# One tag per slot for the big PSUM tiles and the exps tiles of a fused ViT layer

## The chip, the cores and the metric

The kernel runs on one core of one Trainium2 chip. The metric is the device time of one execution in microseconds (us). Before the change, three runs gave 3957.31, 3959.95 and 3960.58 us; the median is 3959.95 us.

## What is computed

A small vision tower: patches are turned into tokens, and one layer with attention and a mixture of experts follows. There are 16 images of 512x512, with 1024 tokens of width 256 each, all in float32. Cut to what matters here:

```python
h = patches(x) @ W.T + b                        # tokens
q, k, v = split(layernorm(h) @ w_qkv)           # 8 heads of 32
k = sum_f a_f * sin(f * k) + b_f * cos(f * k)   # 256 frequencies
attn = softmax(q @ k.T * 32 ** -0.5)
h = h + (attn @ v) @ w_out + b_out
n = layernorm(h)
h = h + shared_mlp(n) + sum of the two best of four experts, weighted by their gates
```

## The kernel before

One long unrolled program handles the 16 images. Its function `plain_path` holds everything that follows; a second path for extreme inputs stands behind a branch and is not taken here.

**The key transform.** The keys of a pair of heads are worked on in 8 groups, 512 groups in all (16 images, 4 pairs of heads, 8 groups). For a group, the angles come in by DMA (`load_waves`, L1072) or are spread by VectorE from one loaded tile (`spread_waves`, L1112). GpSimd multiplies them by the frequencies (`turn_waves`, L1127), ScalarE takes the sines (`sine`, L1136), TensorE weighs them with the coefficients in a *mix* (`mix`, L1156, 16 matmuls into one big PSUM tile called `kan`), and VectorE multiplies the mix by the fast sines (`times_fast`, L1170). TensorE then adds up the products of two groups (`add_up`, L1189, tile `red`), and after four of those the keys of the pair are split and stacked by DMA (`finish_keys`, L1208, and `stack_keys`, L1218).

**Attention.** There are 128 attentions (4 pairs of heads by 2 halves of the queries by 16 images) of 8 chunks `kc` each, so 1024 *scores*. A score (`score`, L1254) is two matmuls into a big PSUM tile `sT` of 128x1024. ScalarE takes the exp (`exponential`, L1270): for an even `kc` it goes to a tile `es` in SBUF, which frees the PSUM tile; for an odd `kc` it stays in place in PSUM. VectorE then adds the odd chunk in PSUM to the even one in SBUF (`pair_sum`, L1285), the result `both` goes to SBUF, and only then is the odd chunk's PSUM tile free. TensorE weighs the values with `es` (8 matmuls) and with `both` (16 matmuls, sums included) in `weigh` (L1300, tile `av`). VectorE divides by the sums (L1324, L1329, L1341).

**The rest.** Tokens, layernorms (VectorE statistics, a chain of small GpSimd steps L621 to L625, ScalarE L633, transposes on TensorE L454), projections and networks are spread between these steps by four chains of generators. They use their own two PSUM slots, `side0` and `side1`, taken through one tag each.

**The slots that the change touches.** Mixes and scores share two PSUM slots of 4 KB per partition: pool `big` (L263) has two buffers under one tag, `big`. `es` and `both` share five SBUF slots: pool `esp` (L258) has NES = 5 buffers under one tag, `es`. With several buffers under a tag, the framework gives a new tile one of the slots when it lays out the program, and makes the tile's first writer wait for the last users of that slot.

**What sets the order of the work.** The order of the instructions of each of the five engines is written out in strings, `ORDERS` (L73 to L225): for TensorE, M is a mix, R an `add_up`, S a score, W a weighting, and digits are steps of the chains. A planner (`run`, L582) walks through them with estimated costs and emits each action. For TensorE, `head` (L564) lets a mix or a score begin in the plan when the user of the last but one big tile is done; the list `bigs` (L1145) holds those users, and `lay_fixed` (L550) adds to it just before the action is called:

```python
at = begin(PE, deps + (bigs[-2:-1] if user_of(token, key) else []))
```

In the same way `tile_free` (L1275) lets an exps tile wait, in the plan, for the weighting of the tile five before it, and for the pair sum too where that one was even.

## Time and profile before

| | |
|---|---|
| median of three runs | 3959.95 us |
| the profiled execution's own time | 3963.14 us |
| its span, first to last instruction | 3961.6 us |
| granted TensorE clock, mean | 0.985 |
| scores, matmuls (L1254) | 2048, 461 ns each |
| mixes, matmuls (L1156) | 8192, 603 ns each |
| exp to `es` (L1270, even chunks) | 512, 1022 ns each |
| exp in place (L1270, odd chunks) | 512, 1012 ns each |
| pair sum (L1285) | 512, 1221 ns each |
| product of a mix (L1170) | 512, 1215 ns each |
| HBM traffic | 230 GB/s over the span |

In the profile, PE is TensorE's matmuls and PEld its weight loads, which overlap with them; DVE is VectorE, ACT ScalarE, POOL GpSimd, SP SyncE. A line such as `av<-es,v` names what is written and what is read. Brackets at the end of a line of the timeline give the idle time of that engine before the instruction and what ended it. In the tables of waits, the columns are the total in us, the number of times, and the longest in us. The first score comes at 142.2 us, the last at 3886.3 us; between some 1000 and 3300 us one image follows the other with a period of about 236 us.

### The profile page before, as it was taken

The numbers are of one execution on the slowest core, as the hardware profiler recorded it, in microseconds if no ns is written. First come the engines' busy times: TensorE is split into PE (matmuls) and PEld (weight loads), VectorE is DVE, ScalarE is ACT, GpSimd is POOL, SyncE is SP. The second block draws the span as 40 slices with busy tenths as digits, with TensorE's granted clock in tenths as the row PEclk, the third lists the DMA queues.
The fourth block names the chain that finished last, engine by engine and source line by source line (L and its number), as shares of the span: only waits on it lengthen the run. The fifth ranks groups of instructions, "written<-read, shape, count | busy, mean of one in ns | idle before, by whom it ended". The sixth has DMA issues, their size and how long they took to land. (4 is left out here: it accounts for less than half of the span.)

```text
span 3961.6 us, 95230 instructions
## 1 busy us (share of the span) xinstructions
PE 3714.6 (94%) x36493; PEld 1784.6 (45%) x36493; DVE 3119.1 (79%) x4715; ACT 3319.6 (84%) x3927; POOL 3193.0 (81%) x2312
## 2 busy tenths in 40 slices
PE   7888999999999999999999999999999999999988
PEld 4324344454444544454454444444454454443434
DVE  4777878878787787878888787887878888797763
ACT  2789988898888888888888888888888898989883
POOL 4988878888888888888888878888888888888850
PEclk9999999999999999999999999999999999999999
DMA  7887977788788788889879788887878878788750
GB/s 241 266 250 210 258 209 230 242 219 273 204 247 253 219 257 224 260 225 252 248 219 279 211 247 243 225 262 215 260 229 247 260 218 261 221 238 232 226 151 18
DMA packets 587586, 916.03 MB, mean 231 GB/s; under 512 B 58828, under 2 KB 177524, under 8 KB 587124
## 3 DMA queue, kind: packets, MB, share of 16 engines
q1 hardware_dynamic: 580880, 906.98, 79.4%
q8 instruction: 291, 4.77, 0.5%
q10 hardware_dynamic: 6244, 2.88, 0.3%
q14 instruction: 171, 1.40, 0.1%
HBM read 758.64 MB, written 150.99 MB: 230 GB/s over the span
## 5 line engine op out<-in xcount | busy, mean ns | idle before, releaser
L1127 POOL TENSOR_TENSOR w<-w,lane 128x1024 int32<-128x1024 int32 x1024 | 1926.8, 1896 | 303.5 <-DMA w<-ud 204.8
L1127 POOL TENSOR_TENSOR f<-f,lane 128x1024 int32<-128x1024 int32 x512 | 970.8, 1896 | 173.1 <-DVE f L1112 131.6
L1136 ACT ACTIVATE w<-w 128x1024 f32<-128x1024 int32 x1024 | 1016.3, 1047 | 57.5 <-POOL w L1127 54.7
L1254 PE MATMUL sT<-q,k 128*128 128x512 f32 x2048 | 739.8, 461 | 138.2 <-ACT es L1270 61.2
L1285 DVE TENSOR_TENSOR both<-sT,es 128x1024 f32<-128x1024 f32 x512 | 625.1, 1221 | 306.0 <-ACT sT L1270 298.7
L1170 DVE TENSOR_TENSOR f<-kan,f 128x1024 f32<-128x1024 f32 x512 | 610.8, 1215 | 162.2 <-ACT f L1136 111.4
L1270 ACT ACTIVATE sT<-sT 128x1024 f32<-128x1024 f32 x512 | 518.0, 1012 | 234.8 <-PE sT L1254 175.4
L1112 DVE STREAM_SHUFFLE f<-src 128x1024 int32<-128x1024 int32 x512 | 691.0, 1362 | 0.9
L1270 ACT ACTIVATE es<-sT 128x1024 f32<-128x1024 f32 x512 | 523.1, 1022 | 105.9 <-PE sT L1254 82.3
L1254 PEld LDWEIGHTS sT<-q,k 128*128 128x128 f32 x2048 | 346.0, 192 | 542.6 <-ACT es L1270 161.8
L1156 PE MATMUL kan<-w,coef 64*32 64x512 f32 x8192 | 558.1, 603 | 31.6 <-ACT w L1136 15.8
L1136 ACT ACTIVATE f<-f 128x1024 f32<-128x1024 int32 x512 | 516.1, 1045 | 0.2
L1300 PE MATMUL av<-both,v 128*32 128x256 f32 x4096 | 324.3, 387 | 3.0 <-DVE both L1285 2.9
L1300 PE MATMUL av<-es,v 128*32 128x256 f32 x4096 | 324.4, 388 | 2.2 <-DVE rc L1341 2.1
L1300 PE MATMUL av<-both,ones 128*32 128x256 f32 x4096 | 320.4, 383 | 0.0
L1189 PE MATMUL red<-f,pack 128*32 128x512 f32 x2048 | 288.2, 605 | 13.4 <-DVE f L1170 13.0
L1324 DVE RECIPROCAL rc<-av 128x256 f32<-128x256 f32 x128 | 224.1, 1751 | 55.4 <-PE av L1300 54.2
L1156 PEld LDWEIGHTS kan<-w,coef 64*32 64x32 f32 x8192 | 119.3, 105 | 303.5 <-issue 114.0
L445 PE MATMUL tok<-wt,x 128*128 128x256 f32 x1008 | 234.7, 384 | 13.8 <-DMA x<-in_xT 12.3
L445 PEld LDWEIGHTS tok<-wt,x 128*128 128x128 f32 x1008 | 189.9, 191 | 61.2 <-issue 21.5
L1136 ACT ACT_TABLE_LOAD x154 | 197.6, 1283 | 21.4 <-DMA w<-ud 18.7
L1300 PEld LDWEIGHTS av<-both,v 128*32 128x32 f32 x4096 | 115.5, 110 | 174.7 <-issue 111.7
(161 smaller groups left out, 4773.3 us busy)
## 6 DMA issues: line engine op xcount, KB each, us to landing
w<-ud SPq DMA_DIRECT2D x2048, 256.0 KB
q<-qd SPq DMA_DIRECT2D x512, 128.0 KB
k<-kd SPq DMA_DIRECT2D x128, 512.0 KB
x<-in_xT SPq DMA_DIRECT2D x128, 384.0 KB
ud<-u SPq DMA_DIRECT2D x64, 512.0 KB
ud<-ui SPq DMA_DIRECT2D x64, 512.0 KB
src<-ud SPq DMA_DIRECT2D x512, 64.0 KB
qd<-qhi SPq DMA_DIRECT2D x64, 256.0 KB
```

The costliest lines, as they stand in the source:

```text
L445: nc.tensor.matmul(out=out, lhsT=lhsT, rhs=rhs, start=start, stop=stop)
L1112: nc.vector.stream_shuffle(w, sources[g // 8].rearrange("p r n -> p (r n)"), [4 * (g % 8) + i // 8 for i in range(32)],)
L1127: nc.gpsimd.tensor_tensor(w, w, f.to_broadcast([P, N]), ALU.mult)
L1136: nc.scalar.activation(x, w, AF.Sin, scale=TURN * 2.0**-32)
L1156: nc.tensor.matmul(out=ps[ds(64 * j + 32 * blk, 32), ts(r, 512)], lhsT=coef[ts(r, 64)].rearrange("p e f j -> p (e f j)"), rhs=w[ts(r, 64), ...
L1170: nc.vector.tensor_mul(w, kan.pop(g), w)
L1189: nc.tensor.matmul(out=rows_of_pair[p][ts(2 * i + r, 32), :], lhsT=pack[:, ds(PACK0 - 16 * (k % 2) - 2 * (k // 2), 32)], rhs=prod[:, ts(r, ...
L1254: nc.tensor.matmul(out=ps[:, ts(s, 512)], lhsT=k4[:, 2 * s + kc // 4, ts(kc % 4, P)], rhs=q4[:, s, :], start=True, stop=True,)
L1270: nc.scalar.activation(es, ps, AF.Exp, scale=SCALE)
L1285: nc.vector.tensor_add(both, scores[kc], exps[kc - 1])
L1300: nc.tensor.matmul(out=acc[0][ts(i, HD), ts(half, 256)], lhsT=ones32 if half else v[:, kc, p % NPAIR, ts(i % 2, HD)], rhs=es[:, ds(512 * ( ...
L1324: nc.vector.reciprocal(rc[0], acc[0][:, 256:512])
```

## The change

The two big slots and the five exps slots each get a tag of their own with one buffer, and the program names the tag. A mix or score takes `big0` and `big1` alternately, by the number of takings so far. An `es` or `both` tile takes slot `(att * NT + kc) % NES`, with NT = 8 chunks per attention. Number and size of the slots stay, as do the instruction orders.

```diff
-    esp = pool("esp", NES)
+    esp = pool("esp", 1)
...
-    big = pool("big", 2, PSUM)
+    big = pool("big", 1, PSUM)
...
-            ps = kan[g] = big.tile([P, N], FP, tag="big", name="kan")
+            ps = kan[g] = big.tile([P, N], FP, tag=f"big{len(bigs) % 2}", name="kan")
...
-            ps = scores[kc] = big.tile([P, 1024], FP, tag="big", name="sT")
+            ps = scores[kc] = big.tile([P, 1024], FP, tag=f"big{len(bigs) % 2}", name="sT")
...
-                es = exps[kc] = esp.tile([P, 1024], FP, tag="es", name="es")
+                es = exps[kc] = esp.tile([P, 1024], FP, tag=f"es{(att * NT + kc) % NES}", name="es")
...
-            both = exps[kc] = esp.tile([P, 1024], FP, tag="es", name="both")
+            both = exps[kc] = esp.tile([P, 1024], FP, tag=f"es{(att * NT + kc) % NES}", name="both")
```

## The prediction

> **What bounds the kernel now.** I read the page's busy times first, then the stretches of one image, then who waited for whom, and last the instructions around the slots.

> ```profile
> PE 3714.6 (94%) x36493; PEld 1784.6 (45%) x36493; DVE 3119.1 (79%) x4715; ACT 3319.6 (84%) x3927; POOL 3193.0 (81%) x2312
> ```
> ```profile
> core 0: us, PE busy (x) PEld busy (x) DVE busy (x) ACT busy (x) POOL busy (x), PEclk, DMA share, GB/s
> 1666.00:1902.00 236.00, 227.85 (x2307) 112.07 (x2306) 195.83 (x296) 203.30 (x244) 199.83 (x144) 0.99 0.86 242
> ```

> In the steady part one image takes 236 us, of which TensorE (PE) is busy 227.85. Only 8.1 us per image is idle there, so a slot rule can win only part of that, and anything that holds PE up costs nearly its full length. The chain that ended last covers only the tail (PE 2% of the span), so I go by PE's waits.

> ```profile
> PE sT L1254 <- ACT es L1270: 61.2, 51, 4.4
> PE sT L1254 <- DVE both L1285: 22.6, 33, 3.0
> PE kan L1156 <- ACT es L1270: 4.6, 7, 1.1
> ```

> The columns are total us, times, longest us. A score (sT) needs no result of an exp. When it waits for one, it waits for the slot that the exp reads. These are the waits that the change touches: 61.2 us in all, the largest row of PE's waits.

> **Which slot is taken now.** The trace has no slot numbers, so I put all 1536 takings of a big slot (512 mixes, 1024 scores) in order of start and gave each the end of its last user: the product (L1170) for a mix, the exp for an even score, the pair sum (L1285) for an odd score. In strict turn, taking n may not start before the user of n-2 is done. 114 takings start earlier, so they took the slot of n-1: 100 are odd score, even score, odd score; 12 are odd score, even score, mix. In the first pattern 187 of some 356 wait on ScalarE's semaphore and 158 on VectorE's, so about half go out of turn. This is one such case:

> ```profile
> 1786.96 1.02 ACT L1270 ACTIVATE es<-sT 128x1024 f32<-128x1024 f32 x1
> 1787.08 1.23 DVE L1285 TENSOR_TENSOR both<-sT,es 128x1024 f32<-128x1024 f32 x1 [0.41 <-ACT sT L1270]
> 1788.21 0.76 PEld L1254 LDWEIGHTS sT<-q,k 128*128 128x128 f32 x4 [0.41 <-ACT es L1270]
> ```

> Two releases run side by side: the even exp ends at 1787.98, the pair sum at 1788.31. The score's weights start at 1788.21, after the exp and before the sum. In turn they would have started after the sum, 0.15 us later. Here is the opposite case:

> ```profile
> 1845.85 1.09 ACT L633 ACTIVATE hn<-h,less,rstd 128x256 f32<-128x256 f32 x2 [2.04 <-POOL less L625]
> 1846.85 1.00 ACT L1270 ACTIVATE es<-sT 128x1024 f32<-128x1024 f32 x1
> 1847.90 0.30 PEld L1254 LDWEIGHTS sT<-q,k 128*128 128x128 f32 x2 [2.61 <-ACT es L1270]
> 1847.91 0.73 PE L1254 MATMUL sT<-q,k 128*128 128x512 f32 x2 [2.42 <-ACT es L1270]
> 1848.57 0.16 PEld L1300 LDWEIGHTS av<-both,v 128*32 128x32 f32 x8 [0.37 <-issue]
> 1848.73 1.01 ACT L1270 ACTIVATE sT<-sT 128x1024 f32<-128x1024 f32 x1 [0.87 <-ACT es L1270]
> 1849.57 0.30 PEld L1254 LDWEIGHTS sT<-q,k 128*128 128x128 f32 x2 [0.41 <-issue]
> ```

> A late layernorm (hn) delays the even exp. The score waits 2.4 us for that exp's slot, though the other slot had been free since 1845.37. The same spot comes in nine images from 1139 to 3032 us, with PE idle 2.3 to 4.4 us each, 27.4 us together.

> [...] weights of a score start up to 0.56 us before the modelled end of the matmuls before. [...]

> **The change part by part.** No instruction of work is added, removed or moved; the orders of all five engines and all DMA issues stay. Only what a taking waits for changes.

> *Big slots, gain.* Where the exp of n-1 comes later than the release of n-2, the score may start earlier. I count 40 takings that start within 0.11 us of n-1's release with n-2 already free; PE idle before them is 31.9 us, of which 27.4 is the nine-fold spot. Not all is won. At 1848 the score (0.73) and the weighting (0.37 for the switch, then 0.64 and 0.61) would fill about 2.0 us; then the next even score needs the slot of that same late exp, and PE waits there for what is left (on average 27.4 / 9 - 2.0 = 1.0). What surely moves is ScalarE: its exp of the score follows the even exp at once, without the 0.87 idle in the last but one line shown. The whole trace has this row:

> ```profile
> ACT sT L1270 <- ACT es L1270: 13.0, 15, 0.9
> ```

> I take these 13.0 us as the gain (15 times 0.87), since PE's next step after the spot, a transpose (lnT), waits for four hn of ScalarE, which move by 0.87 and no more. Bounds: 0 and 31.9.

> *Big slots, loss.* For the 114 out-of-turn takings, end of n-2's user plus 0.05 us (a wait's usual lag, as 1847.85 to 1847.90) minus the start sums to 24.7 us; the median is 0.15, the longest 1.26. Part is covered: where the weights start ahead of the running matmuls, a later start costs nothing until the lead less 0.21 us (load 0.19, gap 0.02) is used up. Taken one by one, 41 with a lead of 0.45 or more lose 0.4 of 9.1 us, 22 with a lead of 0.2 to 0.45 lose 2.4 of 4.4, and the other 51 with hardly any lead, or with PE idle, lose all of their 11.2. The loss is 14.0 us. Bounds: 14.0, and 24.7 if the modelled lead is not real. Behind the waiting score stand the weightings (av), mixes and projections in PE's queue; who waits for it is ScalarE's exp (175.4 us of ACT's idle time is for sT at odd scores), then the pair sum.

> *Even score after an out-of-turn one.* Now it takes the slot of the sum; in turn it takes that of the even exp, which ended earlier or at the same time. I take nothing.

> *Exps slots.* In turn, taking m waits for the release of m-5 (weighting, and for an even tile also the sum). No exp or sum in the trace starts before that; the earliest comes 0.07 us after. 40 takings start within 0.12 us of it; at each of them the four younger tiles still hold the other slots, so that wait is forced either way (ACT es waits for PE av 38 times, 20.0 us). Cost zero, hidden by four younger tiles. An added or dropped EventSemaphore would be 0.05 us; about 100 even exps have one on VectorE now. Bounds: -5 and +5 us.

> *Sum.* How much reaches the end? PE has about ten short stalls per image. Those at 1690 (2.0, keys by DMA) and 1806 (2.0, product after a sine) depend on work that PE itself fed shortly before, so shifts mostly pass; the spot at 1848 depends on POOL's layernorm, and its remaining 1.0 us swallows losses that PE gathered since 1806. I let 0.8 of the gain and 0.65 of the loss through: -10.4 + 9.1 = -1.3 us. The profiled execution took 3963.14 us (span 3961.6 and 1.5 around it), so 3961.8 on its scale; it lies 3.2 above the median of 3959.95, which makes 3958.6, say **3959.0**. With shares from 0.5 to 1 for either, gain and loss give -6.0 to +7.5: 3953 to 3968 is the forecast's own range.

> **Rivals.**
> *Faster.* PE sets the pace, so what counts is PE's idle time: nine times 2.0 refilled and the other 4.5 us of the 31.9, against half the loss: -18.0 - 4.5 + 7.0 = -15.5, 3944. For it: PE is 97% busy in the steady part. Against it: lnT waits for hn.
> *Slower.* The pair sum becomes the only release of each odd score and adds VectorE's queue to PE's path. If the weight lead is only a modelled one, all 24.7 us count, and half of the 13.0 is swallowed: +18.2, 3978. It decides from the point at which the loss let through exceeds the gain by 7.9 us. For it: exp and sum start side by side, and the sum takes 1.22 against 1.02, so it is mostly the later one; it also stands behind reciprocals of 1.75. Against it: 41 of the 114 lie where PE still works for half a microsecond.
> *It does nothing.* If slots went in turn already, no taking could start before n-2 is free. 114 do, so this is left only with a small chance, at 3960.

> **Numbers.** Forecast 0.50, faster rival 0.24, slower rival 0.22, nothing 0.04. About 0.2% (7.9 us) is what a measurement of this kernel can tell from no change, so same is 0.54. The range reaches half into both rivals, with the 5 us of the semaphores: 3945 to 3975.

> **What would show it.** Right: no taking starts before n-2's user ends; "PE sT <- ACT es" falls from 61.2 to about 30 to 45 and "ACT sT <- ACT es" from 13.0 to near zero; "PE sT <- DVE both" rises from 22.6 by up to 14; the stall near 1848 moves to the even score, some 1 us long; "ACT es <- PE av" stays near 20. Wrong: a PE busy share per image that leaves 228 by over 1 us in 236, a new row of waits at L1285 for PE av, or a period that differs from 236 by more than 0.7 us.

## The result and the profile after

The changed kernel takes 3951.56 us in the median, beside 3965.91 us for the kernel before on the same chip, in 20 runs of each. The ratio is 0.9965 with a 95% interval of 0.9953 to 0.9978, so the change saves 0.35%, some 13.9 us (9 to 19). The time lies inside the predicted range of 3945 to 3975, but the range owes that to its width and, in part, to luck: it was laid around 3959.95 us, the median of three runs, and the twenty have a median of 3965.91. The same saving from 3959.95 would give 3946, one microsecond above the lower end. As a change, the forecast was -1.3 us and the measured one is ten times that. The likeliest case, no measurable difference, is not what happened: the kernel became faster, nearly by the -15.5 us of the first rival. The profiled execution took 3944.68 us (span 3943.1), 18.5 us less than the one before; the mean granted clock is 0.989, before 0.985.

The page after, busy time by engine, and then the stretch of one image:

```profile
PE 3710.7 (94%) x36493; PEld 1775.9 (45%) x36493; DVE 3132.7 (79%) x4715; ACT 3317.7 (84%) x3927; POOL 3190.9 (81%) x2312
```
```profile
core 0: us, PE busy (x) PEld busy (x) DVE busy (x) ACT busy (x) POOL busy (x), PEclk, DMA share, GB/s
1666.00:1902.00 236.00, 227.75 (x2307) 111.26 (x2309) 197.32 (x296) 203.27 (x243) 200.08 (x144) 1.00 0.86 243
```

The counts of matmuls, activations and vector instructions are the old ones. PE is busy only 3.9 us less, while the span shrank by 18.5, so the other 14.6 us were time in which the profile has PE idle. A fixed window of 236 us doesn't show this: the kernel now does more than one image in it. The start of one and the same score in images eight apart does: (3144.8 - 1253.5) / 8 = 236.4 us per image before, (3124.1 - 1248.8) / 8 = 234.4 after. Two microseconds over nine images are the whole of the difference between the two profiles.

PE's waits after (line, what ended the wait, us in total, times, longest):

```profile
PE sT L1254 <- ACT es L1270: 37.4, 47, 4.3
PE sT L1254 <- DVE both L1285: 32.5, 51, 3.1
```

The score's wait for an exp fell from 61.2 to 37.4, its wait for a pair sum rose from 22.6 to 32.5. ScalarE's waits at the exps after:

```profile
ACT sT L1270 <- PE sT L1254: 206.3, 222, 5.0
...
ACT es L1270 <- PE av L1300: 22.2, 38, 1.0
...
ACT sT L1270 <- ACT es L1270: 0.9, 1, 0.9
```

The last row was 13.0 us in 15 waits. The middle one, for the exps slot, is where it was (20.0). The nine-fold spot, in the image that was shown before at 1848 us, now looks so (timeline, lines of ScalarE and of PE's matmuls alone):

```profile
1839.16 1.09 ACT L633 ACTIVATE hn<-h,less,rstd 128x256 f32<-128x256 f32 x2 [1.50 <-POOL less L625]
1839.28 0.73 PE L1254 MATMUL sT<-q,k 128*128 128x512 f32 x2
1839.94 0.64 PE L1300 MATMUL av<-both,v 128*32 128x256 f32 x8
1840.16 1.00 ACT L1270 ACTIVATE es<-sT 128x1024 f32<-128x1024 f32 x1
1840.40 0.61 PE L1300 MATMUL av<-both,ones 128*32 128x256 f32 x8
1841.06 1.01 ACT L1270 ACTIVATE sT<-sT 128x1024 f32<-128x1024 f32 x1
1841.21 0.73 PE L1254 MATMUL sT<-q,k 128*128 128x512 f32 x2 [0.20 <-ACT es L1270]
```

The odd score starts at 1839.28, before the even exp (1840.16) has begun. Before, it started only after that exp. ScalarE's exp in place follows the even exp at once (1841.06), where it had an idle 0.87. PE now waits at the next, even score, here 0.20 us. Taken one by one, PE's idle time at the nine odd scores was 27.4 us before and is none after; at the nine even scores behind them it was none and is 10.7 us. PE refills 16.7 us, 1.86 at each spot; the prediction took 2.0.

### The profile page after: what moved, and what is told of

It is laid out like the page before. It is cut to its first block, busy times and chain, and to the rows that moved or that the text cites. A ratio compares the mean times of both kernels' runs of the same rounds, so it can differ in the third digit from the quotient of the medians.

```text
span 3943.1 us, 95385 instructions
## 1 busy us (share of the span) xinstructions
PE 3710.7 (94%) x36493; PEld 1775.9 (45%) x36493; DVE 3132.7 (79%) x4715; ACT 3317.7 (84%) x3927; POOL 3190.9 (81%) x2312
## 5 line engine op out<-in xcount | busy, mean ns | idle before, releaser
L1285 DVE TENSOR_TENSOR both<-sT,es 128x1024 f32<-128x1024 f32 x512 | 625.3, 1221 | 276.5 <-ACT sT L1270 265.5
L1254 PE MATMUL sT<-q,k 128*128 128x512 f32 x2048 | 727.6, 454 | 121.1 <-ACT es L1270 37.4
L1170 DVE TENSOR_TENSOR f<-kan,f 128x1024 f32<-128x1024 f32 x512 | 611.2, 1216 | 154.7 <-ACT f L1136 105.9
L1270 ACT ACTIVATE sT<-sT 128x1024 f32<-128x1024 f32 x512 | 518.1, 1012 | 219.8 <-PE sT L1254 206.3
L1270 ACT ACTIVATE es<-sT 128x1024 f32<-128x1024 f32 x512 | 522.8, 1021 | 100.8 <-PE sT L1254 75.2
L1156 PE MATMUL kan<-w,coef 64*32 64x512 f32 x8192 | 557.1, 603 | 30.5 <-ACT w L1136 13.6
L1254 PEld LDWEIGHTS sT<-q,k 128*128 128x128 f32 x2048 | 340.4, 190 | 537.2 <-DVE both L1285 158.1
L1300 PE MATMUL av<-both,v 128*32 128x256 f32 x4096 | 321.7, 384 | 4.7 <-DVE both L1285 4.7
L1300 PE MATMUL av<-es,v 128*32 128x256 f32 x4096 | 324.0, 387 | 0.9 <-DVE rc L1341 0.9
L1300 PE MATMUL av<-both,ones 128*32 128x256 f32 x4096 | 317.4, 380 | 0.0
L1156 PEld LDWEIGHTS kan<-w,coef 64*32 64x32 f32 x8192 | 118.0, 105 | 302.3 <-issue 109.2
L1300 PEld LDWEIGHTS av<-both,v 128*32 128x32 f32 x4096 | 115.5, 109 | 174.6 <-issue 110.2
```

Of the source, the lines that this page charges most:

```text
L1156: nc.tensor.matmul(out=ps[ds(64 * j + 32 * blk, 32), ts(r, 512)], lhsT=coef[ts(r, 64)].rearrange("p e f j -> p (e f j)"), rhs=w[ts(r, 64), ...
L1170: nc.vector.tensor_mul(w, kan.pop(g), w)
L1254: nc.tensor.matmul(out=ps[:, ts(s, 512)], lhsT=k4[:, 2 * s + kc // 4, ts(kc % 4, P)], rhs=q4[:, s, :], start=True, stop=True,)
L1270: nc.scalar.activation(es, ps, AF.Exp, scale=SCALE)
L1285: nc.vector.tensor_add(both, scores[kc], exps[kc - 1])
L1300: nc.tensor.matmul(out=acc[0][ts(i, HD), ts(half, 256)], lhsT=ones32 if half else v[:, kc, p % NPAIR, ts(i % 2, HD)], rhs=es[:, ds(512 * ( ...
```

## The experiments

Each kernel was timed beside the kernel before on the same chip; the ratios are to that kernel, with 95% intervals, and what stands as an uncertainty or as "within" below is a 95% interval too. No experiment alters what is computed; the dummy matmuls of two of them come on top, and nobody reads their result.

### Each half alone

The big slots by one tag each, the exps slots as before:

```diff
-    big = pool("big", 2, PSUM)
+    big = pool("big", 1, PSUM)
...
-            ps = kan[g] = big.tile([P, N], FP, tag="big", name="kan")
+            ps = kan[g] = big.tile([P, N], FP, tag=f"big{len(bigs) % 2}", name="kan")
...
-            ps = scores[kc] = big.tile([P, 1024], FP, tag="big", name="sT")
+            ps = scores[kc] = big.tile([P, 1024], FP, tag=f"big{len(bigs) % 2}", name="sT")
```

> The two big slots in strict turn, the exps slots as before. Spot theory (the gain comes from the score that waited for a late exp once per image in nine images): the whole gain is here, ratio to the kernel before 0.995 to 0.998. Exps theory (the gain comes from the exps slots): ratio within 0.001 of 1. Spread theory (many small releases of big slots): 0.995 to 0.998 as well, so this run tells only big slots from exps slots.

The exps slots by one tag each, the big slots as before:

```diff
-    esp = pool("esp", NES)
+    esp = pool("esp", 1)
...
-                es = exps[kc] = esp.tile([P, 1024], FP, tag="es", name="es")
+                es = exps[kc] = esp.tile([P, 1024], FP, tag=f"es{(att * NT + kc) % NES}", name="es")
...
-            both = exps[kc] = esp.tile([P, 1024], FP, tag="es", name="both")
+            both = exps[kc] = esp.tile([P, 1024], FP, tag=f"es{(att * NT + kc) % NES}", name="both")
```

> The five exps slots in strict turn, the big slots as before. Spot theory and spread theory: ratio 0.999 to 1.001, since every take of an exps slot in the trace of before starts after the tile five before it is free. Exps theory: 0.995 to 0.998.

Measured: big slots alone 0.9975 (0.9964 to 0.9986), exps slots alone 0.9995 (0.9983 to 1.0007). The big slots carry the gain. The exps slots give nothing that can be measured, although the layout of the compiled kernels shows that the change did alter them: counted by the number `att * NT + kc`, before 97 takings came four after the slot's last taking and 97 six after, and now all come five after.

### The nine spots out, the nine spots in

The same layouts show that the kernel before took 211 of its 1536 big slots out of turn, and the changed one none. The next three kernels choose among the 211. In the first, only the nine spots are taken out of turn as before; everything else is as in the changed kernel:

```diff
+STAYS = {
+    411, 507, 603, 699, 795, 891, 987, 1083, 1179,
+}
...
+    slot = [0]
+
+    def next_slot():
+        if len(bigs) - 1 not in STAYS:
+            slot[0] ^= 1
+        return slot[0]
...
-            ps = kan[g] = big.tile([P, N], FP, tag=f"big{len(bigs) % 2}", name="kan")
+            ps = kan[g] = big.tile([P, N], FP, tag=f"big{next_slot()}", name="kan")
...
-            ps = scores[kc] = big.tile([P, 1024], FP, tag=f"big{len(bigs) % 2}", name="sT")
+            ps = scores[kc] = big.tile([P, 1024], FP, tag=f"big{next_slot()}", name="sT")
```

> The changed kernel, but at nine scores (one in each of nine images, the spot near 1848 us of before) the slot of the last taking is used again, as the kernel before does there. Spot theory: most of the gain is gone, ratio to before 0.999 to 1.001, PE idle 2 to 4 us again at each of the nine, and the period of an image back from 234.4 to 236 us. Spread theory: more than half of the gain stays, ratio at most 0.998.

In the second, STAYS holds the other 202, so that only the nine spots are in turn:

> The kernel before's 211 out-of-turn takings kept, but the nine of the spot put in turn; exps slots in turn. Spot theory: the gain is here, and the small waits for pair sums are not paid, so ratio to before 0.993 to 0.9965, as fast as the changed kernel or up to 9 us faster. Spread theory: less than half of the gain, ratio 0.998 or more.

In the third, a control, STAYS holds all 211: the old assignment, written out by tags.

> All 211 out-of-turn takings of the kernel before, written as a list over the changed kernel, exps slots in turn: the big slots exactly as before. Spot theory: ratio to before 0.999 to 1.001, as with the exps slots alone. If some effect of the tags themselves counted, it would differ by more.

The changed kernel once more, beside the control on the same chip:

> The changed kernel once more, on the chip of the runs beside it. Ratio to before 0.995 to 0.998.

| kernel | nine spots | other 202 | ratio to before |
|---|---|---|---|
| changed | in turn | in turn | 0.9965 (0.9953 to 0.9978) |
| changed, again | in turn | in turn | 0.9970 (0.9959 to 0.9982) |
| spots in | in turn | out | 0.9963 (0.9950 to 0.9976) |
| spots out | out | in turn | 1.0002 (0.9986 to 1.0018) |
| all out | out | out | 0.9990 (0.9975 to 1.0004) |

All three rows with the spots in turn are faster, and neither of the two without. The tags by themselves give nothing (all out, 0.9990). With the others in turn, the nine spots are worth 1.0002 - 0.9970 = 0.0032, 12.7 us, with the others out 0.9990 - 0.9963 = 0.0027, 10.7 us; each difference has an uncertainty of about 0.002. These pairs stand on different chips. On one and the same chip, big slots alone (0.9975) and spots out (1.0002) differ by 0.0027, and spots in (0.9963) and exps slots alone (0.9995) by 0.0032. With the spots out, ScalarE's idle time is back, on the waits of that kernel and on its timeline (the spot of the same image):

```profile
ACT sT L1280 <- ACT es L1280: 7.9, 9, 0.9
```
```profile
1844.00 1.00 ACT L1280 ACTIVATE es<-sT 128x1024 f32<-128x1024 f32 x1
1845.06 0.30 PEld L1264 LDWEIGHTS sT<-q,k 128*128 128x128 f32 x2 [1.48 <-ACT es L1280]
1845.06 0.73 PE L1264 MATMUL sT<-q,k 128*128 128x512 f32 x2 [1.29 <-ACT es L1280]
...
1845.88 1.01 ACT L1280 ACTIVATE sT<-sT 128x1024 f32<-128x1024 f32 x1 [0.87 <-ACT es L1280]
```

The score starts 0.06 us after the exp's end, and its own exp 0.87 after it.

### Is it TensorE's clock?

A rival came up from the traces. Between 1000 and 3200 us the trace before has TensorE's granted clock at one half in 12 windows, eleven of 3.413 us and one of 6.827; the trace after has 3, of 3.413 each. 7 of the 12 begin at one of the nine spots. So PE's stall might cost by what comes after it. This kernel is the one with the spots out, with the stall filled by five dummy matmuls into the free slot:

```diff
+            if len(bigs) - 1 in STAYS:
+                warm = big.tile([P, 1024], FP, tag=f"big{slot[0] ^ 1}", name="warm")
+                for i in range(5):
+                    nc.tensor.matmul(
+                        out=warm[:, ts(i % 2, 512)],
+                        lhsT=k4[:, i % 2, 0:P],
+                        rhs=q4[:, i % 2, :],
+                        start=True,
+                        stop=True,
+                    )
```

> The changed kernel with the nine spots out of turn, and with five extra matmuls of 0.4 us each put ahead of each of the nine waiting scores, written into the other, free slot, where nobody reads them. The score still waits for the late exp; only TensorE's idle time before it is filled. Clock theory (at the spot the idle time lets TensorE's clock fall to half for 3.4 us, and that is most of what the spot costs): no half-clock windows at the nine spots, ratio to before 0.9965 to 0.9985. Queue theory (the spot costs because ScalarE's next exp comes 0.87 us late and TensorE's work lies behind it): filling helps nothing, ratio 0.999 to 1.002.

Measured: 1.0002 (0.9990 to 1.0014). Its timeline at the spot:

```profile
1844.96 1.43 PE L1265 MATMUL warm<-q,k 128*128 128x512 f32 x5
1845.61 1.00 ACT L1290 ACTIVATE es<-sT 128x1024 f32<-128x1024 f32 x1
1846.66 0.73 PE L1274 MATMUL sT<-q,k 128*128 128x512 f32 x2 [0.28 <-ACT es L1290]
1847.48 1.01 ACT L1290 ACTIVATE sT<-sT 128x1024 f32<-128x1024 f32 x1 [0.87 <-ACT es L1290]
```

PE is busy, its idle time at the nine spots is 13.6 us in place of 24.1, and nothing is won: the score still waits for the exp, and ScalarE still idles 0.87. But the run doesn't decide. Its expectation had no half-clock windows left at the nine spots; the trace has them at three, where the kernel with the spots out has six (between 1000 and 3200 us 8 in place of 11). Three windows less are worth about 6 us by the table below, 0.0016, and two ratios of 1.0002 leave an uncertainty of 0.0020 between them.

The traces of all kernels say more. Thirteen traces pass the nine spots 117 times. For each passage I took the time from 10 us ahead of the waiting score to 9 us after its start, by the same two weight loads in every trace, and fitted it with a level for each spot and one for each of four cases. A passage counts as one with a window if over 1 us of that stretch ran at half clock.

| passage of a spot | number | us longer than in turn without a window |
|---|---|---|
| in turn, no half-clock window | 60 | 0 |
| in turn, with a window | 12 | 1.3 (within 0.4) |
| out of turn, no window | 15 | 0.3 (within 0.3) |
| out of turn, with a window | 30 | 2.4 (within 0.3) |

Out of turn a spot is dear where a half-clock window follows, and nearly free where none does. The stalls in the two cases are not the same (2.9 us on average with a window, 1.9 without), but counted from the start of the waiting score, after the stall, the difference is still 1.5 us (within 0.3). Two spots of the kernel with the spots out, first without and then with a window (stretch, its length, busy time of PE, PEld, DVE, ACT and POOL with the numbers of instructions, clock, DMA share, GB/s):

```profile
1845.00:1849.00 4.00, 3.94 (x35) 1.91 (x35) 2.13 (x5) 3.13 (x7) 4.00 (x3) 1.00 1.06 347
2319.00:2323.00 4.00, 4.00 (x25) 2.13 (x18) 2.97 (x8) 2.96 (x6) 3.60 (x5) 0.57 1.07 276
```

In 4 us PE has 35 matmuls at full clock and 25 at a mean clock of 0.57 (the second stretch begins some 1.4 us later in its image, so they are not quite the same ones). Across the three spots of this trace without a window PE is 0.2 us quicker than in the changed kernel, across the six with one 2.0 slower.

So in these traces most of what a spot costs comes with the half-clock window that follows the stall. No experiment moved the clock alone, so this is not shown as the cause. The granted clocks of all timed runs fit it: their median is 0.984 to 0.985 in every kernel with the spots out and not filled, 0.987 to 0.989 with the spots in turn, and among runs of one kernel 10 us more at half clock go with 3.9 us more time (within 0.4, 368 runs). The filled kernel doesn't fit well: its clock is 0.987, by which it should be some 6 us faster than with the spots out, and it is not, with an uncertainty of 8 us.

### PE's lead or ScalarE's exp?

Apart from the clock, the change does two things at a spot: PE gets ahead by a score and a weighting, and ScalarE loses its gap. Three dummy matmuls at the spot of the changed kernel take 1.03 us of PE's lead away and leave ScalarE's part:

```diff
+            if len(bigs) - 1 in SPOTS:
+                warm = big.tile([P, 1024], FP, tag=f"big{slot[0] ^ 1}", name="warm")
+                for i in range(3):
...
```

> The changed kernel (all in turn), with three extra matmuls of 0.4 us ahead of the score at each of the nine spots, into the slot that this score is about to take, where the score overwrites them. The score is still done before the late exp ends, so ScalarE goes from that exp to the next without the 0.87 us of idle time, but TensorE's lead of some 1.7 us shrinks by 1.2 us. If ScalarE's 0.87 us is what the spot gives: ratio to before as the changed kernel, 0.995 to 0.9985. If TensorE's lead is: most of the gain at the spots is lost, 0.9985 to 1.001.

Measured: 0.9977 (0.9966 to 0.9988). Its timeline:

```profile
1840.35 0.97 PE L1264 MATMUL warm<-q,k 128*128 128x512 f32 x3
...
1841.38 0.74 PE L1273 MATMUL sT<-q,k 128*128 128x512 f32 x2
1841.57 1.00 ACT L1289 ACTIVATE es<-sT 128x1024 f32<-128x1024 f32 x1
1842.04 0.64 PE L1319 MATMUL av<-both,v 128*32 128x256 f32 x8
1842.47 1.01 ACT L1289 ACTIVATE sT<-sT 128x1024 f32<-128x1024 f32 x1
```

Measured from the dummies' start, the score is 1.03 us later (1840.35 to 1841.38), but still ahead of its exp, and the two exps remain back to back. Of the changed kernel's 0.0030 to 0.0035, 0.0023 is left; nine times 1.03 us of useless work on PE cost 3 to 5 us, with an uncertainty of 6. Half of the 9.3 us went where PE would have waited anyway: its idle time at the even scores is 5.3 us here, 10.7 in the changed kernel. So most of the gain doesn't hang on PE's full lead. That ScalarE's part is what counts doesn't follow. Two other accounts fit as well. The first is PE's work: PE does useful work in 27.4 - 0.5 - 5.3 - 9.3 = 12.3 us of the old stalls, where the changed kernel does in 16.7, and 12.3 of 16.7 is also about what is left. The second is the clock: eight of the nine spots have no half-clock window here, as in the changed kernel. And ScalarE idles 0.87 in each of the fifteen passages out of turn without a window, which cost 0.3.

### The takings that lose

The changed kernel with the prediction's 114 takings (those that had started early in the trace) out of turn as before, the spots in turn; twice, on two chips:

```diff
+STAYS = {
+    17, 19, 27, 38, 44, 51, 65, 77, 85, 99, 125, 149, 173, 184, 197, 266,
...
+}
```

> The changed kernel, but the 114 takings that started before their turn in the trace of before are let out of turn again; the other 97, the nine spots among them, are in turn. If the waits for pair sums cost what the prediction took (14.0 us, of which 0.65 reaches the end), this is 9 us faster than the changed kernel: 0.992 to 0.995. If these waits are absorbed, it is as fast as the changed kernel: 0.995 to 0.998.

> The changed kernel with the 114 early takings out of turn, once more. If what it gained over the changed kernel before was real, ratio to before 0.993 to 0.9965; if it was the spread of few runs, 0.996 to 0.998 as the changed kernel.

And with the remaining 88 of the 211 out of turn:

> The changed kernel, but the other 88 out-of-turn takings of the kernel before (not the nine spots, not the 114 early ones) are out of turn again. They started, before, when both slots were free or nearly so. If they are neutral: ratio to before as the changed kernel, 0.996 to 0.998. If part of the gain of the change came from them: 0.998 to 1.000.

Measured: 0.9946 (0.9928 to 0.9964) and 0.9962 (0.9949 to 0.9975) for the 114; 0.9980 (0.9969 to 0.9991) for the 88. PE's waits in the second run of the 114:

```profile
PE sT L1271 <- ACT es L1287: 38.2, 46, 4.3
PE sT L1271 <- DVE both L1302: 25.7, 45, 3.1
```

Here the wait for the pair sum is 25.7, nearly the 22.6 of before, and the wait for the exp stays at the new value. The mean of the two is 0.9954, that of the two runs of the changed kernel 0.9968: 0.0014, 5 us, with an uncertainty of as much again. Kernels timed side by side on one chip tell more. The first kernel with the 114 out took 3941.73 us in the median beside 3950.37 for the changed kernel; their means differ by 6.7 us (within 3.8). Spots in, others out took 3946.36 beside 3948.92 for the big slots alone, which differ from them in the 88 and the exps slots too; the means differ by 4.3 (within 4.1). Together that is 5.6 us (within 2.8): putting the early takings in turn does cost time, and the kernel that leaves them out of turn is the faster one. The 0.9980 of the 88 lies on the border of its two cases and doesn't tell them apart.

## Why the prediction was right on the place and wrong on the size

I compared the start of PE's weight loads in each trace with that of the kernel before, instruction by instruction, over the nine images, with the difference at 59 us ahead of the spot taken as zero. The table gives how many us earlier PE is, on average per image:

| kernel | 10 us ahead of the spot | 9 us after it | 95 us after | 176 us after |
|---|---|---|---|---|
| changed | 0.43 | 2.28 | 2.63 | 2.27 |
| changed, again | 0.41 | 1.98 | 2.23 | 1.62 |
| spots in, others out | 0.0 | 1.75 | 2.25 | 2.15 |
| loaded spots | -0.1 | 1.49 | 1.73 | 1.33 |
| 114 out | 0.51 | 2.41 | 2.07 | 1.68 |
| 114 out, again | 0.15 | 2.03 | 3.02 | 3.01 |
| 88 out | 0.86 | 2.49 | 1.97 | 1.77 |
| big slots alone | 0.21 | 2.11 | 1.79 | 1.14 |
| spots out | 1.01 | 1.62 | 0.90 | 0.33 |
| spots out, filled | 0.26 | 1.10 | 0.41 | 0.12 |
| all out | 0.52 | 0.97 | 0.90 | 0.71 |
| exps slots alone (spots out) | 1.00 | 0.63 | 1.66 | 1.68 |

These are single executions. Chance is some tenths across the spot, but over a microsecond by the last column: the exps slots alone stand there at 1.68, as high as the changed kernel, and save nothing that can be measured. What separates the kernels is the step across the spot, second column less first: 1.57 to 1.90 in the eight traces with the spots in turn, -0.37 to 0.84 in the four without, on average 1.76 and 0.38. The difference of 1.4 us times nine is 12 us, as measured.

**What bounds the kernel, and which takings count: right.** The nine spots are the place, and the exps slots and the tags are worth nothing that can be measured. (The 0.05 us that the prediction takes for an EventSemaphore is what the 212 of them at L1254 took in the trace before: 51 ns in the median, up to 3.56 us.) PE's idle time went; with it, in the profiles, went 34 us at half clock (123 before, 90 after), of which the prediction says nothing.

**The gain's raw size: too small, by a row misread.** The prediction took "ACT sT <- ACT es", 13.0 us in 15 waits of 0.87, as the gain, as if the spots stood in it. Listed by time, only four of the nine do (1139, 1376, 1613 and 1848). Nine others are another score some 60 us later in each image, before which PE was not idle. The other five spots stand in a row beside it, on ScalarE's waits of the kernel before:

```profile
ACT sT L1270 <- issue: 32.3, 28, 1.6
```

One of them on its timeline, and then the stretches around it and around 1848 (the last columns are clock, DMA share, GB/s):

```profile
2318.57 1.00 ACT L1270 ACTIVATE es<-sT 128x1024 f32<-128x1024 f32 x1
...
2319.63 1.22 PE L1254 MATMUL sT<-q,k 128*128 128x512 f32 x2 [4.37 <-ACT es L1270]
...
2320.93 1.01 ACT L1270 ACTIVATE sT<-sT 128x1024 f32<-128x1024 f32 x1 [1.36 <-issue]
```
```profile
2319.00:2322.00 3.00, 2.37 (x14) 1.10 (x18) 0.03 (x1) 1.64 (x3) 3.00 (x3) 0.50 1.06 291
1848.00:1851.00 3.00, 3.00 (x30) 1.27 (x31) 1.23 (x2) 2.27 (x5) 3.00 (x3) 1.00 1.06 302
```

The wait is the same, but the score ran at half clock, 1.22 us in place of 0.73, the gap is 1.36 in place of 0.87, and the profile names no releaser for it. Over all nine spots the gap from the even exp's end to the next exp's start is 1.12 us on average before and -0.10 after, since two exps that follow each other overlap by 0.10. So ScalarE's exp moves up by 1.22 us per spot, 11.0 together; with the gaps of the kernel with the spots out (0.87 in eight of nine, 0.93 on average) it is 1.03 per spot, 9.3. The prediction's 0.87 per spot was 7.8.

**What is let through: 0.8, not contradicted.** The prediction expected the next stalls (keys by DMA, the product behind a sine) to swallow a fifth. In the changed kernel nothing is lost from 9 to 176 us after the spot (2.28 and 2.27). But over the eight traces with the spots in turn this change runs from -0.97 to +0.98, on average -0.2 of 1.8. So 0.8 and 1 are not told apart.

**The spots together.** 7.8 times 0.8 made 6.2 us at the end. Two pairs of kernels measured 12.7 and 10.7, on average 11.7, with an uncertainty of about 6. Three counts come near that: ScalarE's move of 9.3 to 11.0, let through whole; PE's idle time (16.7 us less than in the profile before, 24.1 - 10.7 = 13.4 less than in that with the spots out), which was the faster rival's way; and the clock (six spots with a window at 2.4 us and three without at 0.3, together 15, less what the windows left in the changed kernel cost). Only the third fits the passages one by one: ScalarE's gap of 0.87 and a stall of 1.9 us, without a window, cost 0.3. So the step that failed is the price of a spot. The prediction had 0.87 us of ScalarE's time and nothing for the clock; measured is 1.3 us a spot (11.7 / 9), and in the traces the larger part comes with the half-clock window. That this part would be won by the clock alone is not shown.

**The loss: 9.1 us at the end, measured 5.6 (within 2.8).** The early takings do cost time when they are put in turn, by the kernels that ran side by side. The table doesn't show it: 176 us after the spot the two traces with the 114 out stand at 1.68 and 3.01, the changed kernel's at 2.27 and 1.62. The raw 14.0 us and the 0.65 let through are not told apart, and their product was somewhat too large. (The lead of the weight loads, which the prediction gives as up to 0.56 us, reaches 0.59 at the 114 and 1.06 in the whole trace.)

**The sum.** Split at the spots, the prediction was 6.2 us won there and 4.9 lost by all else (9.1 lost, 0.8 of 5.2 won), together -1.3. The runs have 11.7 won at the spots (within 6) and, by the kernel with the spots out, 0.8 lost by all else (within 6), together -10.9; directly measured were -13.9 and, the second time, -11.9, each within about 5. So of the missing 10 to 13 us some 5.5 lie in the spots and 4 in the rest. That the spots carry the gain is shown; how the remainder splits stays rough. A least-squares fit to the times of all kernels without dummies (344 runs, a level for each chip) gives 12.2 us won at the spots, 5.6 lost at the 114, 3.2 won at the 88, for which the prediction took nothing, and 1.6 won at the exps slots, each within 2 to 2.5.

**The signs.** Right: no taking is out of turn; "PE sT <- ACT es" fell into 30 to 45; "ACT sT <- ACT es" fell to 0.9; "PE sT <- DVE both" rose by 9.9; the stall moved to the even score, 10.7 / 9 = 1.2 us on average; "ACT es <- PE av" stayed. The sign that was to show the forecast wrong, a period more than 0.7 us off 236, came: 234.4. As a sign it is weak, since single executions scatter: the exps slots alone have 235.1, the spots out 237.0 where 236 was expected.

## What to carry to other kernels

Where a pool with several buffers under one tag feeds the bounding engine, list its takings by time and look for those that waited for one slot while another was free; a tag for each slot decides the matter, and one such place per iteration can outweigh a hundred short waits (here nine places gave 11.7 us, and 114 waits of 0.15 in the median cost 5.6). Price it occurrence by occurrence and not by a row of totals: here five of nine stood in another row, at another length, where the score ran at half clock (1.22 us in place of 0.73 at 2319 us). Look at the granted clock behind the stall as well as at the stall: here the nine places cost 2.4 us where a half-clock window followed and 0.3 where none did.

## What the runs showed of the hardware

Cut at these multiples, the time from the first score to the last gives 1067 pieces of 3.413 us at full clock before and 1071 after. Sorted by PE's busy share of the piece, they were followed by half clock as often as this:

| PE busy in a piece at full clock | before: pieces, followed by half clock | after: pieces, followed by half clock |
|---|---|---|
| under 40% | 18, 18 | 8, 8 |
| 40 to 60% | 29, 6 | 24, 5 |
| 60% or more | 1020, 0 | 1039, 0 |

Of the pieces at half clock, those with PE busy for 83% or less were followed by another at half clock (4 before, 5 after), and those with 85% or more by full clock (24 before, 13 after). Ends of matmuls are modelled, so the shares are rough.

At 7 of the 9 spots of the kernel before, half clock followed stalls of 2.29 to 4.37 us; five of the seven were shorter than 3.413. At 1613 and 1848 it did not follow the stalls of 3.05 and 2.42 us; each of these lies in two of the pieces, with PE busy for 49% and 55% of the first. The stalls that the change leaves at the even scores are 1.2 us on average, and half clock follows at one of the nine spots.

Over all that the traces record, half clock covers 123 us before and 90 us after.
